# Four graph layers in one kernel: prefix products over two node tiles, a new order of weight tiles at unit boundaries, and copies moved to ScalarE

## The chip, the cores and the metric

The kernel runs on one core of a Trainium2 chip. A core has five engines that work side by side, each on its own queue of instructions: PE (TensorE, matrix products, results in PSUM), DVE (VectorE), ACT (ScalarE, activation functions and copies), POOL (GpSimd) and SP (SyncE). In this kernel SP and POOL issue most of the DMA transfers. Engines wait for each other through semaphores. The metric is the device time of one execution in microseconds (us). Before the change it is 3477.88 us, the median of 3 runs (3473.75 to 3479.8).

## The reference, cut to what matters

There are N = 3327 nodes with 512 features and an adjacency matrix of 0 and 1. Four layers follow each other; each adds its result to its input and normalises every row.

```python
# layers 0, 2 (8 heads of 64) and 3 (4 heads of 128): graph attention
Wh = x @ W                                     # per head
e = leaky_relu(f1[:, :, None] + f2[:, None, :], 0.2)   # f1, f2: Wh times a1, a2
masked = where(adj > 0, e, -9e15)
h = softmax(masked, axis=-1) @ Wh              # layers 2 and 3: then elu
# layer 1: mean over the first 64 neighbours of each node
keep = Ab & (cumsum(Ab, axis=1) <= 64)
nb_mean = (keep @ X) / max(cnt, 1)
y = leaky_relu(X @ W_line.T + b_line) + where(cnt > 0, leaky_relu(nb_mean @ W_nb.T + b_nb), 0)
# after each layer
x = layernorm(x + layer(x))
```

## The kernel before, in words

Nodes are cut into NT = 26 tiles of P = 128 rows; two halves of HALF = 13 tiles (IW = 1664 nodes) are the output halves of an attention layer. The adjacency matrix is loaded once, transposed, and kept on chip as the tile `mask` (one byte for each entry). It arrives in 104 pieces of 128 x 832 integers, which `mask_steps` loads and `mask_set` (line 518) turns into bytes; the first `EARLY` = 88 pieces are handled while layer 0 projects its input, the other 16 beside the first units of layer 0's attention, three in five on DVE and two in five on ACT.

**Projection.** For each tile, `project1` (line 251) transposes the input and `project2` (line 260) multiplies it with W. The products of W with the attention vectors stand in the last columns, so f1 and f2 come out of the same product; ACT copies them into the tile `fc` (line 269). `prepare` (line 293) makes from them, for half of the nodes at a time, a row vector per head (`rd` in memory, over PE transposes `pr` and copies `rr`) and the columns `qc`, `sc` and `bi`; `cut` (line 317) makes bf16 pieces for the sums of the softmax.

**Attention** is done in units (`unit`, line 355): one output half, and one quarter s of the features. In layers 0 and 2 a quarter holds two heads (HS = 2), in layer 3 one (HS = 1). A layer has 8 units. A unit goes over the 26 source tiles j. For each j and each head, DVE makes one weight tile t (line 402, `max` of the row vector `rb` and a column, times the mask) and ACT makes from it a one-byte tile y with a sigmoid (line 405). PE multiplies t with the values `vj` into four banks `po` (line 411), and three tiles later y with `sden` into two banks `pd`, which give the softmax's sums (line 371). Weight tiles have 3 buffers for each head, y tiles 4 (in layer 0 one fewer). The row vectors `rb` of layers 0 and 2 have three buffers; the two of the next unit are loaded by POOL (line 350) as buffers come free.

At the unit's end the four po banks are copied to `ob`, the first by DVE and the others by ACT (lines 426 to 429); four transposes and copies to memory are handed as jobs to the next unit, which does one job after each j. At the end of a half, pd is copied to `db` by both engines (lines 457 to 459), and one of the jobs, `reciprocals` (line 461), multiplies it on PE (`pe`) and takes reciprocals on DVE (lines 474 to 477). Jobs of the first unit of a layer also hold `prepare` and `cut` of the second half.

**Layer 1** is `sage` (line 578). First the input is multiplied with both matrices; the result for the neighbours is cut into three bf16 parts (`zs`, `zl`). Then, for 13 blocks of two output tiles, every pair of block and source tile needs the mask of the first 64 neighbours. ACT writes the count carried from earlier tiles (`cy`, loaded by POOL for four tiles at a time) into one of two PSUM banks `pk` (line 694). PE adds the prefix count of the tile, a product of a triangle of ones with 256 columns of the mask (line 702), and DVE keeps the entries with a count of at most 64 (line 706, `kt`). The kept tiles of the next block are made between the products of this one, ten of them in its first half. PE sums kt times the three parts into `acc` (line 734).

**What sets the order.** PE's instructions run as they are written. On the other engines a planner orders them by estimated costs and due times; an instruction given to `keep_in_program_order` holds its place. Buffers of a pool come free when their last reader is done.

## Time and profile before

| what | value |
| --- | --- |
| median of 3 runs | 3477.88 us |
| the profiled execution | 3476.22 us, its span 3474.4 us |
| busy in the span: PE, DVE, ACT, POOL | 3320.6, 2699.8, 2387.0, 213.3 us |
| mean granted clock of PE | 0.98 |
| line 402, DVE, weight tiles t | 1040, 1959.5 us |
| line 405, ACT, sigmoids y | 1040, 1771.6 us |
| line 411, PE, products po | 8320 records, 1934.8 us |
| line 734, PE, products acc | 645.8 us in two groups |
| lines 694, 702, 706: ACT, PE, DVE on pk | 338 each, 124.0, 92.3, 140.8 us |

All these are from one execution that the hardware profiler recorded. The span runs from its first to its last instruction. A busy time is the time in which an engine had an instruction in work; instructions of one engine can overlap, since PE is pipelined, and a product of 32-bit numbers leaves two records. Behind a group the profile gives the idle time of its engine just before it, and what ended most of it, with an arrow. In a timeline the same stands in brackets. Projection of layer 0 lasts to about 150 us, its attention to about 985, layer 1 to about 1815, layer 2's attention to about 2620, projection and attention of layer 3 to the end.

### The profile page before, as it was taken

The page shows a single profiled execution, that of the slowest core. Times are in us where ns is not written, and L with a number is a line of the kernel's source. Part 1 is how long each engine was busy: PE and PEld are TensorE (multiplying, and loading weights), DVE is VectorE, ACT ScalarE, POOL GpSimd, SP SyncE. Part 2 cuts the span into 40 slices and gives each one's busy share as a digit, 9 for nine tenths or more (in the row PEclk, how much of TensorE's full clock was granted, in tenths as well). Part 3 has the DMA queues.
Part 4 walks back from the last instruction along what each step waited for, and adds up shares of the span by engine and source line. Part 5 has one row for each costly group of instructions (what it writes and reads, how often), then busy time and mean ns, then how long its engine had stood idle before and what let it go on. Part 6 is the DMA issues. An engine that isn't in the chain of part 4 may idle for free.

```text
span 3474.4 us, 48117 instructions
## 1 busy us (share of the span) xinstructions
PE 3320.6 (96%) x18873; PEld 1700.4 (49%) x18926; DVE 2699.8 (78%) x2771; ACT 2387.0 (69%) x2324; POOL 213.3 (6%) x340
## 2 busy tenths in 40 slices
PE   8799999999989999999989999999998999999997
PEld 6544444444444455545554444444446655555553
DVE  6699999999957544344349999999997766668886
ACT  1388988999953343443328999899997655558885
POOL 3100000000010111111110000000001000000000
PEclk9899999999989999999999999999999999999998
DMA  9722111110133422222220111111106511112211
GB/s 382 284 86 68 50 48 47 47 49 28 37 121 122 136 82 68 75 67 69 73 78 18 48 49 47 51 46 43 39 28 205 176 33 44 40 46 91 83 37 47
DMA packets 205354, 276.67 MB, mean 80 GB/s; under 512 B 19325, under 2 KB 140359, under 8 KB 205128
## 3 DMA queue, kind: packets, MB, share of 16 engines
q1 hardware_dynamic: 173464, 164.97, 14.5%
q0 software_dynamic: 26720, 102.65, 9.3%
q10 hardware_dynamic: 4944, 5.98, 0.5%
q8 instruction: 149, 2.44, 0.3%
q14 instruction: 77, 0.63, 0.1%
HBM read 204.92 MB, written 68.60 MB: 79 GB/s over the span
## 4 chain that ended last, share of the span: by engine, by line
PE 59%; issue 27%; DVE 6%; DMA 5%; ACT 2%; POOL 1%; ACTq 0%; POOLq 0%; SPq 0%; DVEq 0%
PE po L411 33%; PE acc L734 9%; PE pd L371 4%; PE pw L265 4%; DVE t L402 3%; DMA raw<-in_adjT_dram 3%; PE pz L623 3%; PE pi L626 2%; PE pt L435 1%; ACT y L405 1%; DMA cy<-ctd 1%; PE pk L702 1%; DVE kt L706 1%; PE pe L466 1%; PE pt L254 1%
## 5 line engine op out<-in xcount | busy, mean ns | idle before, releaser
L402 DVE SCALAR_TENSOR_TENSOR t<-rb,qc,mask 128x1664 f32<-128x1664 f32 x1040 | 1959.5, 1944 | 191.7 <-PE po L411 154.4
L405 ACT ACTIVATE y<-t,bi,sc 128x1664 fp8e4<-128x1664 f32 x1040 | 1771.6, 1766 | 339.1 <-PE pd L371 324.5
L411 PE MATMUL po<-t,vj 128*64 128x448 f32 (+3 forms) x8320 | 1934.8, 521 | 23.8 <-DVE t L402 23.5
L411 PEld LDWEIGHTS po<-t,vj 128*64 128x64 f32 (+1 forms) x8320 | 856.4, 148 | 972.8 <-issue 676.3
L734 PE MATMUL acc<-zs,kt 128*128 128x512 bf16 x1314 | 394.7, 380 | 1.5
L265 PE MATMUL pw<-wsb,xT 128*128 128x264 f32 (+1 forms) x1248 | 301.8, 397 | 18.6 <-DVE vt L271 15.6
L734 PEld LDWEIGHTS <-kt 128*128 128x128 fp8e4 x2028 | 198.2, 98 | 226.4 <-issue 29.8
L694 ACT CAST pk<-cy 128x256 f32<-128x256 bf16 x338 | 124.0, 374 | 268.2 <-DVE kt L706 220.5
L265 PEld LDWEIGHTS pw<-wsb,xT 128*128 128x128 f32 x1248 | 240.7, 197 | 62.9 <-issue 14.1
L371 PE MATMUL pd<-y,sden 128*32 128x448 fp8e4 (+1 forms) x4160 | 259.7, 342 | 10.5 <-ACT y L405 10.5
L706 DVE SCALAR_TENSOR_TENSOR kt<-pk,mask 128x256 fp8e4<-128x256 f32 x338 | 140.8, 420 | 157.2 <-PE pk L702 156.6
L734 PE MATMUL acc<-zl,kt 128*128 128x512 bf16 x661 | 251.1, 380 | 1.4 <-DMA zl<-zd 0.8
L371 PEld LDWEIGHTS <-sden 128*32 128x32 bf16 x4160 | 117.7, 96 | 162.4 <-issue 139.7
L269 ACT COPY fc<-pw 128x8 f32<-128x8 f32 (+1 forms) x156 | 23.6, 162 | 148.2 <-PE pw L265 148.2
L271 DVE TENSOR_TENSOR vt<-pw,dc 128x256 f32<-128x256 f32 x156 | 58.7, 417 | 80.8 <-ACT dc L266 76.6
L350 POOL DMA_DIRECT2D rb<-r x40 | 21.2, 532 | 1617.0 <-DVE t L402 1610.2
L702 PE MATMUL pk<-mask,upto 128*128 128x256 fp8e4 x338 | 92.3, 273 | 19.9 <-ACT pk L694 18.9
L526 DVE TENSOR_SCALAR mask<-raw 128x832 fp8e4<-128x832 int32 (+2 forms) x98 | 58.4, 603 | 51.0 <-DMA raw<-in_adjT_dram 50.7
L623 PE MATMUL pz<-wn,xT 128*128 128x512 f32 x208 | 96.1, 606 | 1.3 <-ACT xT L617 1.3
L626 PE MATMUL pi<-wl,xT 128*128 128x512 f32 x208 | 93.5, 592 | 0.0
L592 POOL DMA_DIRECT2D cy<-ctd x91 | 67.8, 745 | 395.9 <-ACT pk L694 267.8
L714 DVE SCALAR_TENSOR_TENSOR y<-acc,cnt,bnb 128x512 f32<-128x512 f32 x26 | 19.5, 751 | 83.5 <-PE acc L734 83.5
(167 smaller groups left out, 1750.7 us busy)
## 6 DMA issues: line engine op xcount, KB each, us to landing
vj<-v SPq DMA_DIRECT2D x312, 128.0 KB
rb<-r POOLq DMA_DIRECT2D x40, 832.0 KB, 4.7
raw<-in_adjT_dram SPq DMA_DIRECT2D x71, 416.0 KB
cy<-ctd POOLq DMA_DIRECT2D x78, 256.0 KB, 3.9
h<-hd SPq DMA_DIRECT2D x65, 256.0 KB
hd<-hb SPq DMA_DIRECT2D x60, 256.0 KB
v<-vt SPq DMA_DIRECT2D x50, 256.0 KB
xr<-x POOLq DMA_DIRECT2D x45, 256.0 KB, 3.2
```

The lines of the kernel that those rows point to most:

```text
L265: nc.tensor.matmul(pw[e][:, :FW + H], xT[:, c, :], wsb[:, c, e, :], start=c == 0, stop=c == FC - 1)
L371: nc.tensor.matmul(pd[c][32 * kk:32 * kk + 32, :w_], lhsT, rhs, start=(kk, c) not in seen, skip_group_check=final is not None, stop=last a ...
L402: nc.vector.scalar_tensor_tensor(t, rb[k], self.qc[:, j, h:h + 1], mask[:, j, i0:i0 + IW], op0=ALU.max, op1=ALU.mult)
L405: nc.scalar.activation(y, t, AF.Sigmoid, bias=self.bi[:, j, h:h + 1], scale=self.sc[:, j, h:h + 1], saturate=False)
L411: nc.tensor.matmul(po[c][k * D:(k + 1) * D, :z - a_], vj[:, j % 2, k * D:(k + 1) * D], ts[k][:, a_:z], start=j == 0, stop=j == NT - 1)
L592: nc.gpsimd.dma_start(out=cy[:, :n, :], in_=ctd[t:t + n, b * GW:(b + 1) * GW] .rearrange("(o t) i -> o t i", o=1).to_broadcast([P, n, GW]))
L623: nc.tensor.matmul(pz, xT[:, c, :], wn[:, c, :], start=c == 0, stop=c == FC - 1)
L626: nc.tensor.matmul(pi, xT[:, c, :], wl[:, c, :], start=c == 0, stop=c == FC - 1)
L694: nc.scalar.copy(pks[k % 2], carry[b, t // 4 * 4][:, t % 4, :])
L702: nc.tensor.matmul(pk, upto, mask[:, t, i0:i0 + GW], start=False, stop=True, skip_group_check=True)
L706: nc.vector.scalar_tensor_tensor(kt, pk, NEIGHBOURS, mask[:, t, i0:i0 + GW], op0=ALU.is_le, op1=ALU.mult, saturate=False)
L734: nc.tensor.matmul(acc, kts[t][:, s * P:(s + 1) * P], zs(t, c) if c < 2 else zl[:, t, :], start=t == 0 and c == 0, stop=t == NT - 1 and c ...
```

## The change

- **Prefix products for two tiles at once.** In `sage`, a pk bank holds two tiles next to each other; copy, product and selection work on 128 x 512 instead of 128 x 256, and there are 169 of each instead of 338. The pool of kt has half as many buffers of twice the size. Ahead of need, pairs are made after every fourth tile in a block's first half and every second in its second.
- **Order of heads.** In layers 0 and 2, for the first two and the last two source tiles of a unit, both weight tiles of head 0 are made before both of head 1. Between them the order stays.
- **Copies by ScalarE.** In layers 0 and 2, ACT does all four ob copies and all four db copies.
- **Sums and reciprocals.** The products pe are a job of their own, and the reciprocals follow two tiles later, with their first multiplication on DVE held in program order. In the last unit of all, pe is put into a po bank and stands behind the first two groups of transposes.
- **f1 and f2 in place.** The tile fc is gone; the copies go to rc and qc, and prepare works there.
- **Second half's preparation.** In layers 0 and 2, two empty jobs stand ahead of prepare and cut of the second half, and their first DVE instructions are held in program order.
- **The mask's start.** 82 instead of 88 pieces are handled in the projection. The first 8 pieces, not 4, are loaded through ACT's queue, and the four weight tiles of `attend` have four buffers there.
- **The last stores** go from the highest tile of each group to the lowest.

```diff
@@ project2, prepare, cut @@
-                nc.scalar.copy(self.fc[:, t, e * H:(e + 1) * H], pw[e][:, FW:FW + H])
+                nc.scalar.copy((self.rc, self.qc)[e][:, t, :], pw[e][:, FW:FW + H])
...
-            nc.vector.tensor_scalar(rc, f1, RCLAMP, -RCLAMP, op0=ALU.min, op1=ALU.max)
+            ins = nc.vector.tensor_scalar(rc, rc, RCLAMP, -RCLAMP, op0=ALU.min, op1=ALU.max)
+            if pinned:
+                tc.keep_in_program_order(ins)
...
-                nc.vector.tensor_copy(pc[:, :, :, c0], dc)
+                ins = nc.vector.tensor_copy(pc[:, :, :, c0], dc)
+                if pinned:
+                    tc.keep_in_program_order(ins)
@@ unit @@
+            def weights(j, k):
+                h = heads[k]
+                t = tp.tile([P, IW], F32, name="t")
+                nc.vector.scalar_tensor_tensor(t, rb[k], self.qc[:, j, h:h + 1],
+                                               mask[:, j, i0:i0 + IW], op0=ALU.max, op1=ALU.mult)
+                y = yp.tile([P, IW], F8, name="y")
+                nc.scalar.activation(y, t, AF.Sigmoid, bias=self.bi[:, j, h:h + 1],
+                                     scale=self.sc[:, j, h:h + 1], saturate=False)
+                return t, y
...
+                if HS == 1 or j not in (1, NT - 1):
+                    made = {}
+                    for k in range(HS):
+                        for j_ in (j, j + 1) if HS > 1 and j in (0, NT - 2) else (j,):
+                            made[j_, k] = weights(j_, k)
+                ts, ys = zip(*(made[j, k] for k in range(HS)))
...
-                if c:
+                if c or HS == 2:
                     nc.scalar.copy(ob[:, a_:z], po[c][:, :z - a_])
...
-                nc.vector.tensor_copy(db[64:, c * (WB // 2):(c + 1) * (WB // 2)], pd[c][64:, :WB // 2])
+                (nc.scalar.copy if HS == 2 else nc.vector.tensor_copy)(
+                    db[64:, c * (WB // 2):(c + 1) * (WB // 2)], pd[c][64:, :WB // 2])
...
-            return jobs[:2] + [reciprocals] + jobs[2:]
+            if final and s == NS - 1:
+                take = []
+                return [lambda: take.append(transposed(*QUADS[0])), lambda: take.append(transposed(*QUADS[1])),
+                        sums, reciprocals] + [lambda q=q: take[q]() for q in range(2)] + \
+                    [lambda q=q: transposed(*q)() for q in QUADS[2:]]
+            return jobs[:2] + [sums, nothing, reciprocals] + jobs[2:]
@@ sage @@
-                    tc.tile_pool(name="sb_k", bufs=NT + 10, reuse_waits="tile") as kp, \
+                    tc.tile_pool(name="sb_k", bufs=NT // 2 + 5, reuse_waits="tile") as kp, \
...
-                pks = [pkp.tile([P, GW], F32, name=f"pk{i}") for i in range(2)]
+                pks = [pkp.tile([P, 2, GW], F32, name=f"pk{i}") for i in range(2)]
...
-                order = [(b, t) for b in range(len(blocks)) for t in range(NT)]
+                order = [(b, t) for b in range(len(blocks)) for t in range(0, NT, 2)]
...
-                        nc.scalar.copy(pks[k % 2], carry[b, t // 4 * 4][:, t % 4, :])
+                        nc.scalar.copy(pks[k % 2], carry[b, t // 4 * 4][:, t % 4:t % 4 + 2, :])
...
-                    nc.tensor.matmul(pk, upto, mask[:, t, i0:i0 + GW], start=False, stop=True,
+                    nc.tensor.matmul(pk, upto, mask[:, t:t + 2, i0:i0 + GW], start=False, stop=True,
                                      skip_group_check=True)
                     carry_in(k + 1)
-                    kt = kp.tile([P, GW], F8, name="kt")
-                    nc.vector.scalar_tensor_tensor(kt, pk, NEIGHBOURS, mask[:, t, i0:i0 + GW],
+                    kt = kp.tile([P, 2, GW], F8, name="kt")
+                    nc.vector.scalar_tensor_tensor(kt, pk, NEIGHBOURS, mask[:, t:t + 2, i0:i0 + GW],
                                                    op0=ALU.is_le, op1=ALU.mult, saturate=False)
...
-                            if not last and (len(ahead) < 10 and t % 2 == 1 and b > 0 if s == 0 else
-                                             len(ahead) < min(NT, t + 11)):
-                                ahead.append(kept(b + 1, len(ahead)))
+                            if not last and (len(ahead) < 10 and t % 4 == 1 and b > 0 if s == 0 else
+                                             len(ahead) < min(NT, t + 10) and t % 2 == 1):
+                                ahead += kept(b + 1, len(ahead))
@@ the end of layer 3 @@
-                    for q in range(qs.start, qs.stop):
+                    for q in reversed(range(qs.start, qs.stop)):
@@ layer 0 @@
-            EARLY = 3 * NT + 10
-            msteps = mask_steps(rw0, pieces[:EARLY], 5, (), False, 4)
+            EARLY = 3 * NT + 4
+            msteps = mask_steps(rw0, pieces[:EARLY], 5, (), False, 8)
...
-                wt = pool.tile([P, F], F32, name="wt", tag=tag)
+                wt = pool.tile([P, F], F32, name="wt", tag=tag, bufs=FC if tag == "wt" else 1)
...
-                return [lambda: L0.prepare(f0, 1, "xr", 1), lambda: L0.cut(f0, 1, "h", 2)] + count_jobs(pool, 0)
+                return [lambda: None] * 2 + [lambda: L0.prepare(f0, 1, "xr", 1, True), lambda: L0.cut(f0, 1, "h", 2, True)] + \
+                    count_jobs(pool, 0)
```

Layer 2's first jobs change in the same way as layer 0's. In the tail, `final` returns its DVE and ACT part as a function `take` for the last unit, so that it can be called after the reciprocals.

## The prediction

> **What bounds the kernel now.** I read the windows first (busy time of each engine by stage), because the page's PE share of 96% is an average over stages with different limits. Columns: length, then busy us (instructions) of PE, weight loads, DVE, ACT, POOL; granted clock; DMA share; GB/s. The rows are the projection of layer 0, the first unit of its attention, a unit of layer 2, the mean layer (layer 1), a unit of layer 3.
>
> ```profile
> 50.00:150.00 100.00, 86.54 (x411) 71.68 (x409) 64.81 (x149) 21.16 (x88) 24.55 (x40) 0.97 1.01 380
> 150.00:200.00 50.00, 38.46 (x267) 14.87 (x269) 46.46 (x54) 30.14 (x22) 1.07 (x3) 0.83 0.27 78
> 2030.00:2130.00 100.00, 98.17 (x692) 44.63 (x690) 99.35 (x55) 92.02 (x60) 1.06 (x2) 1.00 0.14 44
> 1600.00:1700.00 100.00, 96.58 (x471) 52.58 (x479) 44.00 (x107) 41.49 (x95) 14.08 (x21) 1.00 0.25 74
> 3020.00:3105.00 85.00, 85.00 (x334) 42.73 (x333) 56.20 (x34) 48.38 (x32) 0.53 (x1) 1.00 0.14 42
> ```
>
> So the projection is held by DMA (share 1.01), the mean layer and layer 3 by PE. In layers 0 and 2 both PE and DVE read full, and DVE's order in time decides which it is. It shows a unit boundary as copy, wait, then 52 weight tiles without a hole:
>
> ```profile
> 2020.74 0.61 DVE L429 COPY ob<-po 128x448 f32<-128x448 f32 x1
> 2022.00 96.94 DVE L402 SCALAR_TENSOR_TENSOR t<-rb,qc,mask 128x1664 f32<-128x1664 f32 x52 [0.66 <-DMA rb<-r]
> 2118.86 0.61 DVE L429 COPY ob<-po 128x448 f32<-128x448 f32 x1
> 2120.13 96.94 DVE L402 SCALAR_TENSOR_TENSOR t<-rb,qc,mask 128x1664 f32<-128x1664 f32 x52 [0.65 <-DMA rb<-r]
> ...
> 2235.11 0.21 DVE L474 TENSOR_TENSOR rec<-pe,rc 128x52 f32<-128x52 f32 x1 [2.38 <-PE pe L466]
> ```
>
> A weight tile takes 96.94/52 = 1.865 us of DVE, two tiles of nodes 7.46. PE needs 5.9 for their products and 0.9 for their sums, 6.8, and follows. ACT's timeline has four sigmoids in 6.77, 88 us a unit, and with the copies 92. So layers 0 and 2 are DVE's: each DVE microsecond taken away there is a microsecond, until PE or ACT is reached some 5 us a unit lower.
>
> In the mean layer PE is full except where the prefix product waits for ScalarE to put the carried counts into its bank:
>
> ```profile
> 1366.03 0.38 PE L734 MATMUL acc<-zl,kt 128*128 128x512 bf16 x1
> 1367.37 0.27 PE L702 MATMUL pk<-mask,upto 128*128 128x256 fp8e4 x1 [0.96 <-ACT pk L694]
> 1367.48 0.59 PE L734 MATMUL acc<-zs,kt 128*128 128x512 bf16 x2
> ```
>
> An acc product starts 0.215 after the one before it. Here 1.34 pass, so 1.13 are lost; with three smaller holes beside it (0.10, 0.17, 0.19) a block of 46.1 us loses 1.59.
>
> **The change, part by part** (minus is a gain).
>
> *Copies leave DVE in layers 0 and 2.* The ob copy keeps DVE 0.54 (2118.86 to the wait; 0.61 with its overlap). 14 units are followed by another of their layer: 14 x 0.54 = 7.6. The two db copies between the halves, 1.06 (1.03 and a gap), twice: 2.1. Together -9.7. At each layer's end nothing overlaps: two db copies join ScalarE's row, about 0.95 (its own pair there takes that), twice: +1.9. A boundary gives ScalarE 0.5 more, 92.5 against some 97: hidden.
>
> *Order of heads.* The second row vector of a unit is loaded into the buffer that head 0 of the unit before leaves. Between its last use and its need lie today two weight tiles, the copy and the wait: 2 x 1.865 + 0.54 + 0.65 = 4.9, which is what the load takes (4.7 to landing). In the new order two tiles of the old unit and two of the new lie between, 7.5, so the waits go: 0.69, 1.65, 0.68, 0.22 in layer 0 and 0.37, 0.66, 0.65, 0.81 in layer 2: -5.7. What is late instead is PE: the last but one tile and the next unit's first get their second head one weight tile (1.865) later. PE's wait is hidden as long as the six weight buffers last; the third rival prices this.
>
> *Sums apart from reciprocals.* DVE stood 2.66 (layer 0) and 2.38 behind the pe products, with all weight tiles queued behind it. The reciprocals come two tiles later and are held in program order, when pe is long done: -5.0. PE's 26 products (3.35) stay and are inside its slack. In layer 3 DVE has slack: nothing.
>
> *Six mask pieces leave the projection.* 6 x 426 kB = 2.56 MB, at the 0.40 MB per us of its saturated rows 6.4 us. Loading the fourth weight tile without a buffer wait lets PE start earlier (today it waits for that load 8.40 at 19.79), but DMA is full anyway. Bounds 0 (then PE, busy 87%, is the pace) and -8 (the first 10 us moved 254 GB/s and fill up too); nearer the row of bytes: -5. The pieces come back in layer 0: three more on DVE at 0.50, +1.5, and three on ScalarE at 0.9, hidden.
>
> *Second half's preparation pinned behind six weight tiles.* Today DVE does some 5 us of it before layer 0's first weight tile and PE stands 9.35; it then stalls 3.47 on PE in layer 0 and 0.60 in layer 2. Afterwards that work lies between weight tiles: the same DVE time, a shorter hole on PE. Against it stand two things. ScalarE now needs Exp between sigmoids: two table switches per layer. The trace's row is
>
> ```profile
> L405 ACT ACT_TABLE_LOAD x35 | 44.9, 1283 | 15.2 <-DVE t L402 8.7 <-PE pd L371 5.9
> ```
>
> that is 2 x 1.28 = 2.6 a layer. [...] The trace has the first sigmoid 0.02 after the load's end (158.02 + 1.28, next at 159.32), so I take the row. And three of the four rr copies now stand nearly in a row, each behind the store of the one before (2.76 in layer 0); no sigmoid between them. ScalarE then lags some 12 us behind DVE; six buffers (11.2) and the 5 us of preparation on DVE just cover that. Its four stores move two slots down SP's queue, behind vj loads that have four buffers; their rows are read three units later. [...] Bounds -4 (both stalls gone) and +8 (ScalarE's lag uncovered); taken -1, as the row of the stall is the nearest.
>
> *Pairs in the mean layer.* A 256-column product starts 0.108 before its successor (1363.72 to 1363.83), a 512-column acc 0.215, so 338 x 0.108 = 169 x 0.215: PE gains nothing by itself. The copies and selections halve in number (ACT 0.374 to about 0.56, DVE 0.42 to about 0.7, by the 512-wide rows of this page), off the path. What counts is the loop copy, product, selection on one of two banks. Today it has 1.51 us (two tiles) and needs 0.37 + 0.27 + 0.42 and gaps, 1.2 to 1.3; a table load with the Sqrt (1.58) or an output step breaks it. With pairs it has 3.0 and needs 1.9, so 1.1 of slack for 0.25. Of 1.59 lost per block some 0.6 stay: 11 x 1.0 = 11, and 1 in the first four products. The first block also waits for the carries' DMA (cy, 3.9 to landing, two buffers); that stays. Bounds 0 and -18; taken -12.
>
> *The rest.* f1 and f2 in place: as many copies, same width: 0. Layer 3 has HS = 1, its order and copies stay: 0. The end: transposes ahead of the pe products (fill PE's 1.10 wait, push pe by 0.9), stores reversed so that the two-part last tile isn't the last: -0.5, between -2 and +1.
>
> Sum: -9.7 + 1.9 - 5.7 - 5.0 - 5.0 + 1.5 - 1.0 - 12.0 - 0.5 = **-35.5**. The profiled execution took 3476.2 (span 3474.4 and 1.8 around it), 1.7 under the median of 3477.9; I take the sum off the median: **3442**.
>
> **Rivals.** *Holes stay in the mean layer.* The carry loads or the table loads remain what ends the wait, and pairs only make it coarser. For it: cy waits are 45.4 us of ScalarE's; against it: they lie mostly in the first block. Price +12: 3454.
>
> *ScalarE takes over in layers 0 and 2.* Its sigmoids already wait for PE's release of the y buffers, 324.5 us in all, and every copy moved lands in its row. If it can't catch up after a boundary, the gain of copies, rows and reciprocals (-20.4 + 1.9 = -18.5) is given back: 3461. Against it: 92 busy of 100.
>
> *Slower: PE late at every boundary.* Count from the start of a unit's last four weight tiles. PE starts tile 24 at 5.6, ends tile 25 at 5.6 + 2 x 2.92 = 11.4, the last sums at 13.1 to 13.8, the next unit's tile 0 (complete at 13.1) at 16.0 to 16.7, tile 1 at 18.9 to 19.6. DVE needs the buffer of tile 1's first head for its twelfth weight tile, at 11 x 1.865 = 20.5. So 0.9 to 1.6 are left; what PE is later, DVE loses, 14 times. To turn -35.5 into a loss it takes 35.5/14 = 2.5 us beyond that slack. What could do it: in some units of layer 0 the ob copies stand ahead of the last sigmoid on ScalarE, whose y the last sums need. At 3 us beyond: 3442 + 42 = 3484.
>
> *Nothing to see:* the first two rivals together and the stage's start failing, about 3475.
>
> **How the numbers follow.** As forecast 0.71 (own range 3430 to 3450), mean layer 0.12, ScalarE 0.10, nothing 0.03, PE at boundaries 0.04. Low end: every part at its good bound, -9.7 + 1.9 - 5.7 - 5.0 - 8 - 4 - 18 - 2 = -50.5, the masks' 1.5 hidden in it: 3427. High end 3461, through the first rival to the second. A change under 0.2% (7 us) can't be told from none here. Faster 0.93, same 0.03, slower 0.04.
>
> **What would show it.** DVE's timeline in layers 0 and 2: units of 52 x 1.865 = 97.0 end to end with no ob and no rb wait between (98.1 today), no wait on pe. Projection's last mask near 143 instead of 150. Blocks of 45 instead of 46.1 in the mean layer and no pk wait near 1 us. Layer 3 units at 83 as before. It is wrong if DVE shows waits for PE or ACT after each boundary, if pk still waits, or if layer 0's first unit is longer than its 114 (156 to 270) by more than the 6.5 us of work moved into it.

## The result, and the profile after

The changed kernel takes 3434.9 us (median of four runs, 3434.6 to 3437.3); the kernel before, run beside it, 3478.3 (four runs). The ratio is 0.9879, with an interval from 0.9862 to 0.9896: 43.4 us less. The forecast was 3442, between 3427 and 3461. The profiled executions took 3434.62 (span 3432.9) and 3476.22 (span 3474.4), so the spans differ by 41.5.

The forecast's terms can be sorted by stage and set beside what each stage gave. The stages are cut in the timelines by the first and the last weight tile of a layer (t), and in the mean layer by the first acc product and the first and last output row. The third column is a second profile of the unchanged kernel, described below: it tells how far a stage repeats.

| stage | before, us | before once more | forecast | changed kernel |
|---|---|---|---|---|
| start to layer 0's first t | 156.0 | -2.8 | -10.0 (5 of it only moved) | -11.5 |
| layer 0, first to last t | 813.5 | -2.2 | -5.0 (with 5 moved in) | -8.4 |
| to the mean layer's first acc | 225.4 | -2.5 | +1.0 | -7.1 |
| first acc to first output row | 26.1 | +1.5 | -1.0 | **+7.0** |
| first to last output row | 579.4 | +0.2 | -11.0 | -14.2 |
| to layer 2's first t | 19.2 | -0.7 | 0 | -0.6 |
| layer 2, first to last t | 792.7 | +0.3 | -10.0 | -12.5 |
| to layer 3's first t | 137.7 | +0.3 | +1.0 | **+5.1** |
| layer 3, first to last t | 684.4 | 0.0 | 0 | **+2.6** |
| to the end | 40.1 | -0.3 | -0.5 | -1.9 |
| sum | 3474.4 | -6.2 | -35.5 | -41.5 |

(The forecast for layer 0 is -3.8 for ob copies, -1.0 for db copies, -3.2 for row waits, -2.7 for pe, +1.5 for masks, -0.8 of the one microsecond for the preparation, and +5 for what moves in; for layer 2 it is -3.8, -1.0, -2.5, -2.4 and -0.2.) So the sum was nearly right, but three stages lost 14.7 us where the forecast had zero for the three together, and the others gained 56.2 where it had 35.5.

The windows of the changed kernel (columns as before: length, busy us and instructions of PE, weight loads, DVE, ACT, POOL; granted clock, DMA share, GB/s), for the projection, layer 0's start, a unit of layer 2, the mean layer and a unit of layer 3:

```profile
50.00:140.00 90.00, 78.08 (x370) 63.77 (x369) 58.82 (x134) 19.55 (x79) 24.13 (x38) 0.96 1.03 390
140.00:190.00 50.00, 40.53 (x276) 17.57 (x276) 48.66 (x59) 36.05 (x29) 1.26 (x3) 0.90 0.33 103
1990.00:2090.00 100.00, 99.94 (x706) 47.51 (x704) 100.00 (x55) 93.46 (x63) 1.06 (x2) 1.00 0.14 44
1575.00:1675.00 100.00, 99.22 (x466) 52.24 (x465) 40.36 (x74) 37.92 (x68) 15.36 (x22) 1.00 0.27 77
2968.00:3051.00 83.00, 83.00 (x328) 41.71 (x327) 53.28 (x31) 46.55 (x30) 0.53 (x1) 1.00 0.14 43
```

The bounds are where they were. In layer 2 DVE now reads exactly 100 of 100, and ScalarE 93.5 with the copies (92.0 before). PE in the mean layer is full to 99.2 (96.6 before). DVE's timeline of layer 2 shows the boundaries gone altogether:

```profile
1811.25 383.75 DVE L398 SCALAR_TENSOR_TENSOR t<-rb,qc,mask 128x1664 f32<-128x1664 f32 x206
2194.92 0.20 DVE L493 TENSOR_TENSOR rec<-pe,rc 128x52 f32<-128x52 f32 x1
...
2201.70 363.26 DVE L398 SCALAR_TENSOR_TENSOR t<-rb,qc,mask 128x1664 f32<-128x1664 f32 x195
```

206 weight tiles over four boundaries take 383.75, that is 1.863 each, with no wait in brackets; the reciprocals start without waiting for pe. A unit is 52 x 1.863 = 96.9, as forecast (97.0). Layer 0's first unit, into which 6.5 us of work moved, takes 114.6 (112.5 before), and the projection's last mask step starts at 143.97 (forecast: near 143). And in a block of the mean layer the pk product stands in line with no wait, where 0.96 was lost before:

```profile
1384.87 0.38 PE L759 MATMUL acc<-zl,kt 128*128 128x512 bf16 x1
1385.08 0.38 PE L727 MATMUL pk<-mask,upto 128*128 128x512 fp8e4 x1
1385.30 0.59 PE L759 MATMUL acc<-zs,kt 128*128 128x512 bf16 x2
```

Most blocks take 44.8 to 45.1 (46.1 before; forecast 45). Between the first and the last output row two waits for pk are left, 0.80 and 0.45, where there were twelve of 0.96 or more before. The page's two rows for the pairs (mean ns of one after "busy,") are 0.587 and 0.688, near the 0.56 and 0.7 that were estimated:

```profile
L719 ACT CAST pk<-cy 128x512 f32<-128x512 bf16 x169 | 98.4, 587 | 289.3 <-DVE kt L731 231.5
L731 DVE SCALAR_TENSOR_TENSOR kt<-pk,mask 128x512 fp8e4<-128x512 f32 x169 | 116.1, 688 | 109.2 <-PE pk L727 108.5
```

### The profile page after: what moved, and what is told of

Its sections match the earlier page's. It is cut to its first block, busy times and chain, and to the rows that moved or that the text cites. A ratio compares the mean times of both kernels' runs of the same rounds, so it can differ in the third digit from the quotient of the medians.

```text
span 3432.9 us, 47500 instructions
## 1 busy us (share of the span) xinstructions
PE 3298.5 (96%) x18757; PEld 1660.5 (48%) x18757; DVE 2670.2 (78%) x2575; ACT 2378.1 (69%) x2182; POOL 213.4 (6%) x340
## 4 chain that ended last, share of the span: by engine, by line
PE 71%; issue 13%; DMA 7%; DVE 5%; ACT 3%; POOL 1%; SPq 0%; POOLq 0%; ACTq 0%; DVEq 0%
PE po L421 49%; PE pd L373 7%; PE acc L759 4%; DVE t L398 3%; DMA raw<-in_adjT_dram 3%; PE pz L648 3%; PE pi L651 3%; DMA cy<-ctd 3%; PE pw L264 2%; ACT y L401 1%; PE pt L445 1%; DMA h<-hd 1%; POOL cy L617 1%; PE pa L957 0%; PE pe L480 0%
## 5 line engine op out<-in xcount | busy, mean ns | idle before, releaser
L421 PE MATMUL po<-t,vj 128*64 128x448 f32 (+3 forms) x8320 | 1913.9, 521 | 25.1 <-DVE t L398 24.8
L421 PEld LDWEIGHTS po<-t,vj 128*64 128x64 f32 (+1 forms) x8320 | 835.4, 148 | 975.0 <-issue 713.0
L759 PE MATMUL acc<-zs,kt 128*128 128x512 bf16 x1352 | 405.2, 382 | 0.0
L719 ACT CAST pk<-cy 128x512 f32<-128x512 bf16 x169 | 98.4, 587 | 289.3 <-DVE kt L731 231.5
L264 PEld LDWEIGHTS pw<-wsb,xT 128*128 128x128 f32 x1248 | 240.8, 197 | 56.2 <-issue 5.3
L731 DVE SCALAR_TENSOR_TENSOR kt<-pk,mask 128x512 fp8e4<-128x512 f32 x169 | 116.1, 688 | 109.2 <-PE pk L727 108.5
L268 ACT COPY rc<-pw 128x8 f32<-128x8 f32 (+1 forms) x78 | 12.7, 163 | 142.6 <-PE pw L264 142.6
L651 PE MATMUL pi<-wl,xT 128*128 128x512 f32 x208 | 93.5, 592 | 0.0
L551 DVE TENSOR_SCALAR mask<-raw 128x832 fp8e4<-128x832 int32 (+2 forms) x95 | 55.5, 594 | 44.8 <-DMA raw<-in_adjT_dram 44.5
L256 DVE TENSOR_REDUCE xsum<-xT 128x4 f32<-128x512 f32 x78 | 53.0, 681 | 39.2 <-ACT xT L255 38.8
```

Source lines behind the costliest of these rows:

```text
L264: nc.tensor.matmul(pw[e][:, :FW + H], xT[:, c, :], wsb[:, c, e, :], start=c == 0, stop=c == FC - 1)
L421: nc.tensor.matmul(po[c][k * D:(k + 1) * D, :z - a_], vj[:, j % 2, k * D:(k + 1) * D], ts[k][:, a_:z], start=j == 0, stop=j == NT - 1)
L651: nc.tensor.matmul(pi, xT[:, c, :], wl[:, c, :], start=c == 0, stop=c == FC - 1)
L719: nc.scalar.copy(pks[k % 2], carry[b, t // 4 * 4][:, t % 4:t % 4 + 2, :])
L731: nc.vector.scalar_tensor_tensor(kt, pk, NEIGHBOURS, mask[:, t:t + 2, i0:i0 + GW], op0=ALU.is_le, op1=ALU.mult, saturate=False)
L759: nc.tensor.matmul(acc, kts[t][:, s * P:(s + 1) * P], zs(t, c) if c < 2 else zl[:, t, :], start=t == 0 and c == 0, stop=t == NT - 1 and c ...
```

## The experiments

Questions: does each part give its term, why does the mean layer's start lose 7, and where do layer 3's losses come from? The theory is the forecast's: layers 0 and 2 are DVE's, every DVE microsecond taken away is a microsecond, the mean layer is PE's. The rivals are ScalarE or a late PE at the boundaries.

| run | median, us | kernel before beside it | ratio (interval) |
|---|---|---|---|
| e_pairs | 3465.2 | 3477.2 | 0.9967 (0.9952 to 0.9981) |
| e_heads | 3469.7 | 3477.2 | 0.9975 (0.9968 to 0.9983) |
| e_copies | 3476.9 | 3477.2 | 1.0000 (0.9991 to 1.0008) |
| e_sums | 3474.4 | 3477.2 | 0.9993 (0.9985 to 1.0002) |
| e_headcopy | 3459.2 | 3474.5 | 0.9962 (0.9947 to 0.9977) |
| e_start | 3473.4 | 3474.5 | 0.9996 (0.9987 to 1.0005) |
| e_unpin | 3440.6 | 3474.5 | 0.9908 (0.9892 to 0.9925) |
| e_carry | 3429.7 | 3475.8 | 0.9868 (0.9853 to 0.9882) |
| e_best | 3429.4 | 3475.8 | 0.9865 (0.9850 to 0.9880) |
| e_best_end | 3431.2 | 3475.8 | 0.9872 (0.9856 to 0.9889) |
| e_five | 3458.1 | 3475.8 | 0.9949 (0.9934 to 0.9964) |

Beside the first four, 37 runs of the kernel before spread from 3471.1 to 3487.7. A part worth 3 us is therefore read from the stages of its trace, and the time only has to agree.

### The kernel before, once more

The same program, unedited.

> The kernel before, once more, to see how far its stages repeat. Between the last weight tile of layer 2 and the first of layer 3 its profile had 137.7 us; the changed kernel and the four kernels with one part of the change each had 140.4 to 142.8, though most of them change nothing there. If these stages scatter from one execution to the next, this profile has some other number between 137 and 143; if each program has its own, 137.7 comes back, and so do 202.5 from the mean layer's first product to its first acc product and 684.4 for layer 3's weight tiles.

One run, 3470.0 us. Its stages are the third column of the table above. Those that hang on DMA scatter by 2 to 3 us (the projection, layer 0, the passage to the mean layer); the passage to layer 3 came back as 138.0, layer 3 as 684.4. So the kernel before repeats in these two, and +5.1 and +2.6 are more than its scatter; the changed kernel was profiled once.

### Pairs alone

```diff
-                pks = [pkp.tile([P, GW], F32, name=f"pk{i}") for i in range(2)]
+                pks = [pkp.tile([P, 2, GW], F32, name=f"pk{i}") for i in range(2)]
...
-                order = [(b, t) for b in range(len(blocks)) for t in range(NT)]
+                order = [(b, t) for b in range(len(blocks)) for t in range(0, NT, 2)]
...
-                        nc.scalar.copy(pks[k % 2], carry[b, t // 4 * 4][:, t % 4, :])
+                        nc.scalar.copy(pks[k % 2], carry[b, t // 4 * 4][:, t % 4:t % 4 + 2, :])
```

> Before with the pairs of the mean layer alone. The prediction's term: 12 us faster, all of it between the mean layer's first and last output rows (578.7 us apart before), because a block loses 0.6 instead of 1.6. What the trace of the changed kernel suggests instead: 14 us are gained between these rows (564.5), and some 7 are lost ahead of the first of them, because ScalarE's pairs put the load of the third group of carried counts ahead of layer 2's weights on POOL's queue: then this kernel is about 7 us faster in all, its first output row comes 33 us after its first acc product (26.1 before), and the two loads of wsb are issued after the first pk product, not 18 us ahead of it. If the 7 us come from another part of the change, this kernel is 14 us faster and its first output row comes at 26.

12.0 us faster by the medians (6.6 to 16.7 by the interval). From the first output row to the last 15.3 less, from the first acc product to the first row 6.0 more (26.1 to 32.0). Both halves of the second reading hold; together the two stages give 9.3, and the time alone cannot tell 7 from 12. PE's timeline of this run at the start of the mean layer has two large waits:

```profile
1195.96 0.58 PE L734 MATMUL acc<-zl,kt 128*128 128x512 bf16 x1 [5.20 <-DMA zl<-zd]
1207.37 0.38 PE L702 MATMUL pk<-mask,upto 128*128 128x512 fp8e4 x1 [3.16 <-ACT pk L694]
```

So the pairs themselves bring the loss at the start; which mechanism, e_carry decides.

### Order of heads alone

```diff
-                for k, h in enumerate(heads):
-                    t = tp.tile([P, IW], F32, name="t")
...
+                if HS == 1 or j not in (1, NT - 1):
+                    made = {}
+                    for k in range(HS):
+                        for j_ in (j, j + 1) if HS > 1 and j in (0, NT - 2) else (j,):
+                            made[j_, k] = weights(j_, k)
+                ts, ys = zip(*(made[j, k] for k in range(HS)))
```

> Before with the order of heads at a unit's ends alone. The prediction's term: 5.7 us faster; the waits of DVE for rb (5.7 us in eight boundaries of layers 0 and 2) are gone, all else as before, the ob copy and the pe waits too. Rival (PE late at boundaries): what rb gave comes back as waits of DVE for PE (po) after each boundary, and the time is the same or longer.

7.5 us faster (5.9 to 11.1 by the interval). Layer 0 is 4.0 shorter and layer 2 1.9: 5.9 against 5.7. No wait for rb is left and no wait for PE follows a boundary, so the rival falls. One thing grew: DVE's stall on PE in the first unit is 4.1 in layer 0 and 1.6 in layer 2 (3.5 and 0.6 in the first profile of before, 1.9 and 1.0 in the second), because PE's first pair of weight tiles is complete one tile later.

### Copies alone

```diff
-                if c:
+                if c or HS == 2:
                     nc.scalar.copy(ob[:, a_:z], po[c][:, :z - a_])
...
-                nc.vector.tensor_copy(db[64:, c * (WB // 2):(c + 1) * (WB // 2)], pd[c][64:, :WB // 2])
+                (nc.scalar.copy if HS == 2 else nc.vector.tensor_copy)(
+                    db[64:, c * (WB // 2):(c + 1) * (WB // 2)], pd[c][64:, :WB // 2])
```

> Before with the ob and db copies of layers 0 and 2 on ScalarE alone. The prediction's term: 9.7 less 1.9 = 7.8 us faster. But the row vector's load now has 0.54 us less between its buffer's release and its need, as the copy stood between: if the load is what ends the wait, the eight rb waits grow by 0.54 each and the rest of the boundaries get one, and of 7.6 us at most 3 show; then this kernel is 2 to 4 us faster. If ScalarE takes over, DVE waits for y or for PE after each boundary and nothing shows.

0.3 us faster, between 3.1 faster and 2.8 slower: the term of 7.8 did not come. DVE's timeline of this run at two boundaries of layer 2:

```profile
2009.03 7.53 DVE L402 SCALAR_TENSOR_TENSOR t<-rb,qc,mask 128x1664 f32<-128x1664 f32 x4
2017.46 96.94 DVE L402 SCALAR_TENSOR_TENSOR t<-rb,qc,mask 128x1664 f32<-128x1664 f32 x52 [0.89 <-DMA rb<-r]
2115.55 5.68 DVE L402 SCALAR_TENSOR_TENSOR t<-rb,qc,mask 128x1664 f32<-128x1664 f32 x3 [1.16 <-PE po L411]
```

The first and the last row are cut by the window. The copy is gone and the wait behind it is longer (0.66 before at the first of the two). Over eight boundaries, four in each layer, waits grew from 6.0 to 9.9 us, half of the 7.6 that the ob copies took. The row vector arrives when it arrives, and the copy had been part of the wait for it. (At the second boundary PE's release of a weight buffer came last.) Layers 0 and 2 are 1.2 and 1.9 shorter, so the copies did give 3.1 there; the passage to layer 3 is 3.1 longer, and why is open. Whether ScalarE would allow the full gain is left to the next run.

### Heads and copies together

The two edits above.

> Before with the order of heads and the ob and db copies on ScalarE, both. Alone, the order of heads gave 7.5 us and the copies 0.3. If the copies' gain was held back only by the row vector's load (the new order gives it 7.5 us), DVE now has neither wait nor copy at a boundary of layers 0 and 2: from a layer's first to its last weight tile layer 0 takes 813.5 - 3.2 - 3.7 - 1.0 = 805.5 and layer 2 792.7 - 2.5 - 3.7 - 1.0 = 785.5, and the kernel is 13 to 15 us faster. If ScalarE is what holds the copies back, the two only add: 8 us faster, with waits for y or po at the boundaries.

15.3 us faster by the medians (8.0 to 18.4 by the interval). Layer 0 takes 805.5, as expected; layer 2 783.1, for which 785.5 was expected. Its DVE timeline runs over four boundaries of layer 2 without a wait:

```profile
1826.65 389.36 DVE L396 SCALAR_TENSOR_TENSOR t<-rb,qc,mask 128x1664 f32<-128x1664 f32 x209 [1.53 <-PE po L419]
2217.20 0.21 DVE L483 TENSOR_TENSOR rec<-pe,rc 128x52 f32<-128x52 f32 x1 [1.18 <-PE pe L475]
```

The copies, worth 0.3 alone, are worth 15.3 - 7.5 = 7.8 behind the new order. That this equals the forecast's -9.7 + 1.9 is partly luck: the two intervals are wide, and by the stages layers 0 and 2 are 4.0 and 7.7 shorter than with the order alone. Of these 11.7 us 1.7 are a shorter wait for pe (1.92 and 1.18 where the order alone has 2.38 twice), so some 10 are the copies'. In layer 2 no weight tile waits for ScalarE, and in layer 0 such waits grow by 0.6, so that rival falls.

### Sums apart from reciprocals, alone

```diff
-            def reciprocals():
+            def sums():
...
+            def reciprocals():
+                pe = held[0]
...
+                    tc.keep_in_program_order(
+                        nc.vector.tensor_tensor(r_[:, :, k, ss], pv[:, :, 0, k, ss], rc[:, :, k, ss], op=ALU.mult))
...
-            return jobs[:2] + [reciprocals] + jobs[2:]
+            return jobs[:2] + [sums, nothing, reciprocals] + jobs[2:]
```

> Before with sums and reciprocals as two jobs, two slots apart, and the reciprocals pinned (layers 0, 2 and 3; the end of layer 3 keeps its order). The prediction's term: 5.0 us faster (waits of 2.66 in layer 0 and 2.38 in layer 2 are gone). Rival: the wait is only moved, to the first weight tile behind it, because PE is 3.35 us of sums behind: then the same time, with waits for po in its place.

2.8 us faster (5.2 faster to 0.7 slower). Layer 0 is 2.35 shorter and layer 2 2.51, both waits for pe are gone and no new one stands there: 4.9 of 5.0. But layer 3 is 2.5 longer, where the forecast had zero. Two things make this up. At the boundary behind the second unit of its second half PE waits longer for the last sigmoid. ScalarE's order differs there: between its last two activations of the tile e (line 185) it makes one sigmoid, and before it made two. PE's timeline of the kernel before, and of this run:

```profile
3270.91 0.54 PE L371 MATMUL pd<-y,sden 128*32 128x448 fp8e4 x6 [0.92 <-ACT y L405]
```

```profile
3268.24 0.54 PE L371 MATMUL pd<-y,sden 128*32 128x448 fp8e4 x6 [1.78 <-ACT y L405]
```

That is 0.86. The other 1.7 are a stretch at a lower granted clock just behind the pe products (5 us at 0.66 lose 5 x 0.34): the next eight products po take 4.73 there, and 3.04 in the kernel before, where the clock reads 1.00. The windows of this run, and of e_best where the split is undone in layer 3, at the same place (last three columns: clock, DMA share, GB/s):

```profile
3280.00:3285.00 5.00, 5.00 (x18) 2.27 (x17) 2.61 (x5) 1.32 (x1) 0.20 (x1) 0.66 0.18 52
```

```profile
3240.00:3245.00 5.00, 5.00 (x24) 2.52 (x24) 3.48 (x6) 2.74 (x2) 0.20 (x1) 1.00 0.25 79
```

### Projection's start alone

```diff
-            EARLY = 3 * NT + 10
-            msteps = mask_steps(rw0, pieces[:EARLY], 5, (), False, 4)
+            EARLY = 3 * NT + 4
+            msteps = mask_steps(rw0, pieces[:EARLY], 5, (), False, 8)
...
-                wt = pool.tile([P, F], F32, name="wt", tag=tag)
+                wt = pool.tile([P, F], F32, name="wt", tag=tag, bufs=FC if tag == "wt" else 1)
```

> Before with the projection's start alone: six mask pieces later, eight loads from ScalarE's queue, a buffer for each tile of transposed weights. The prediction's terms: layer 0's first weight tile 5 us sooner (151 in place of 156; between 156 and 148), the layer 1.5 longer by three more mask pieces on DVE: 3.5 us faster. The changed kernel's first weight tile came at 144.5, of which the preparation that it moved behind it explains some 5; so 149.5 would be the rest.

1.1 us faster (4.5 faster to 1.7 slower). The first weight tile comes at 150.4, 5.6 sooner than in the first profile of before and 2.8 sooner than in the second; layer 0 is then 1.0 or 3.2 longer. The sign and the rough size hold; with stages that scatter by 3 us the exact term is not to be had from one trace.

### The preparation where it was

```diff
-                return [lambda: None] * 2 + [lambda: L0.prepare(f0, 1, "xr", 1, True), lambda: L0.cut(f0, 1, "h", 2, True)] + \
-                    count_jobs(pool, 0)
+                return [lambda: L0.prepare(f0, 1, "xr", 1), lambda: L0.cut(f0, 1, "h", 2)] + count_jobs(pool, 0)
...
-                L2.attention(rp, lambda pool, half, s: [lambda: None] * 2 +
-                             [lambda: L2.prepare(mp, 1, "rr", 1, True), lambda: L2.cut(mp, 1, "pc", 1, True)]
+                L2.attention(rp, lambda pool, half, s: [lambda: L2.prepare(mp, 1, "rr", 1), lambda: L2.cut(mp, 1, "pc", 1)]
```

> The changed kernel with the second half's preparation of layers 0 and 2 where it stood before (next to the first weight tiles, not pinned). The prediction's term: 1 us slower, with 4 slower (DVE's stall of 3.5 on PE in layer 0's first unit and of 0.6 in layer 2's is back) and 8 faster (ScalarE's lag behind the pinned preparation) as its bounds. The trace of the changed kernel shows no wait in that place, which speaks for 4 slower.

3440.6 us: 5.7 slower than the changed kernel by the medians, 10 by the ratios, whose intervals leave a wide margin. DVE's timeline of this run at the start of layers 0 and 2:

```profile
149.22 14.98 DVE L398 SCALAR_TENSOR_TENSOR t<-rb,qc,mask 128x1664 f32<-128x1664 f32 x8
168.81 1.95 DVE L398 SCALAR_TENSOR_TENSOR t<-rb,qc,mask 128x1664 f32<-128x1664 f32 x1 [4.60 <-PE po L421]
...
1809.18 3.81 DVE L398 SCALAR_TENSOR_TENSOR t<-rb,qc,mask 128x1664 f32<-128x1664 f32 x2 [1.86 <-PE po L421]
```

The stalls are 4.60 and 1.86, not 3.47 and 0.60. In the changed kernel both are zero: 6.5 us, and the stages from the start to layer 0's end and in layer 2 are 5.0 + 1.9 = 6.9 longer here. ScalarE's timeline of the changed kernel tells what the pinned preparation cost there:

```profile
158.05 1.28 ACT L300 ACT_TABLE_LOAD   x1
159.35 0.29 ACT L300 ACTIVATE rc<-rc 128x104 f32<-128x104 f32 x1
159.66 1.28 ACT L401 ACT_TABLE_LOAD   x1
160.95 1.77 ACT L401 ACTIVATE y<-t,bi,sc 128x1664 fp8e4<-128x1664 f32 x1
```

Two loads of 1.28, and after each the next activation starts within 0.02. DVE does not wait for ScalarE in these first units (in the changed kernel neither from 145 to 250 nor from 1785 to 1880).

### The carried counts' load behind the weights

```diff
-                nc.gpsimd.dma_start(out=cb, in_=ctd[NT:NT + 1, :].rearrange("o (t p) -> p (o t)", p=P))
+                cbl = nc.gpsimd.dma_start(out=cb, in_=ctd[NT:NT + 1, :].rearrange("o (t p) -> p (o t)", p=P))
...
-                            load_carry()
+                            with tc.issue_after(cbl.ins) if k == 2 else nullcontext():
+                                load_carry()
```

> The changed kernel with the load of the third group of carried counts queued on POOL behind the two loads of wsb, bnb and cb, as it stood before. In the changed kernel and in the run of the pairs alone it stands ahead of them and is free only when ScalarE has copied two pairs, so the 1 MB of wsb is issued 1.2 us after the first acc product (23 us ahead of it before) and shares the DMA engines with the first zl tiles: PE waits 4.64 for zl and 4.16 for the carried counts. If that is the cause of the 6 to 7 us between the first acc product and the first output row, these come 26 to 28 apart again and the kernel is 5 to 7 us faster, near 3429. If the pairs themselves are (a pair of counts or of masks later), they stay 33 apart.

3429.7 us, 5.2 less than the changed kernel. POOL's timeline of the kernel before, of the changed kernel, and of this run:

```profile
1171.85 0.80 POOL L143 DMA_DIRECT2D wsb<-in_w_dram  x1 [27.93 <-DVE xi L637]
1174.60 0.77 POOL L143 DMA_DIRECT2D wsb<-in_w_dram  x1 [1.95 <-issue]
...
1194.14 0.76 POOL L592 DMA_DIRECT2D cy<-ctd  x1 [7.89 <-ACT pk L694]
```

```profile
1166.14 0.80 POOL L617 DMA_DIRECT2D cy<-ctd  x1 [48.99 <-ACT pk L719]
1169.07 1.51 POOL L143 DMA_DIRECT2D wsb<-in_w_dram  x2 [2.13 <-DVE kt L731]
1170.57 0.55 POOL L695 DMA_DIRECT2D bnb<-in_bn_dram  x1
```

```profile
1143.94 0.80 POOL L143 DMA_DIRECT2D wsb<-in_w_dram  x1 [27.82 <-DVE xi L662]
1146.69 0.77 POOL L143 DMA_DIRECT2D wsb<-in_w_dram  x1 [1.95 <-issue]
...
1164.66 0.76 POOL L617 DMA_DIRECT2D cy<-ctd  x1 [6.34 <-ACT pk L720]
```

In the changed kernel a load of counts stands first whose buffer ScalarE frees only at 1166; the 1 MB of weights behind it was issued 1.2 us after the first acc product (1167.84) instead of 23 ahead of it. PE's waits at the mean layer's start, in the changed kernel and in this run:

```profile
1173.07 0.58 PE L759 MATMUL acc<-zl,kt 128*128 128x512 bf16 x1 [4.64 <-DMA zl<-zd]
...
1184.64 0.58 PE L727 MATMUL pk<-mask,upto 128*128 128x512 fp8e4 x1 [4.16 <-ACT pk L719]
```

```profile
1171.41 0.59 PE L760 MATMUL acc<-zl,kt 128*128 128x512 bf16 x1 [4.67 <-DMA zl<-zd]
...
1182.45 0.38 PE L728 MATMUL pk<-mask,upto 128*128 128x512 fp8e4 x1 [0.90 <-ACT pk L720]
```

From the first acc product to the first row it is 26.4 again (33.1 in the changed kernel). So it is in the two runs built on this edit (26.4 and 26.6), while the two other variants of the changed kernel, without it, have 32.9 (e_unpin) and 31.4 (e_five). By the time alone 5.2 would not be certain, as the two ratios' intervals overlap. The cause is shown, with one correction to the expectation: the wait for zl stays as in the changed kernel, so the weights did not delay the first zl tile. They delayed the counts behind them: the next load of counts is issued at 1172.59 there and lands 11.2 us later, here at 1166.98 and 7.6. PE's wait for them falls from 4.16 to 0.90. After two waits in a row PE also ran the next 17 us at a granted clock of 0.81 (1184 to 1201), where this run has 1.00 from 1182 on. The 3.3 of the wait and the 3.2 of the clock (17 x 0.19) are the 6.6. Why PE waits 4.7 for zl with the pairs and 0.76 without them stays open.

### Layer 3 as before, and the layers' ends as before

The run before, and:

```diff
+                    if HS == 2:
+                        tc.keep_in_program_order(ins)
...
+            if HS == 1:
+                return jobs[:2] + [lambda: (sums(), reciprocals())] + jobs[2:]
             return jobs[:2] + [sums, nothing, reciprocals] + jobs[2:]
```

> As the run before, and in layer 3 sums and reciprocals are one job again and not pinned (its last unit keeps the changed order). Split and pinned they cost layer 3's weight tiles 2.5 us in the run of the split alone (684.4 to 686.9) and 2.6 in the changed kernel. If that is the split's doing, layer 3's weight tiles are back at 684.4 and this kernel is 2.5 us faster than the run before.

3429.4 us: 0.3 less than e_carry, where 2.5 were expected. Layer 3 is back at 684.4 (and PE's wait of 1.78 at 0.92), but the passage from layer 2 to layer 3 took 144.6 in this program (142.5 in e_carry) and the projection 2.2 more. The edit does what it says; in the time it can't be told from none.

Then the second edit on top, which leaves one ob copy and two db copies of a layer's last unit on DVE:

```diff
-                if c or HS == 2:
+                if c or HS == 2 and not ending:
...
-                (nc.scalar.copy if HS == 2 else nc.vector.tensor_copy)(
+                (nc.scalar.copy if HS == 2 and not ending else nc.vector.tensor_copy)(
```

> As the run before, and at the end of layers 0 and 2, where no weight tiles follow, one ob copy and two db copies go back to DVE. The prediction's term: the copies in a row on ScalarE cost 0.95 at each of the two ends, so 1.9 us faster; if they are what makes the passage from layer 2 to layer 3 take 142.8 instead of 137.7, 5 us faster. If that passage is longer for other reasons (the runs of the pairs and of the sums alone, which change nothing there, had 142.1 and 140.4), 0 to 2 us.

3431.2 us, no gain, and the passage to layer 3 still takes 142.8. So the copies in a row on ScalarE are not what lengthens it, and the term of +1.9 for them isn't visible.

### Five weight buffers

```diff
-            with tc.tile_pool(name="at_t", bufs=3 * self.HS, reuse_waits="tile") as tp, \
+            with tc.tile_pool(name="at_t", bufs=3 * self.HS - (self.HS == 2), reuse_waits="tile") as tp, \
```

> The changed kernel with five weight buffers instead of six in layers 0 and 2, to measure how near the rival of a late PE was. By the prediction's count PE has 0.9 to 1.6 us to spare at each of 14 boundaries; one buffer less takes one weight tile, 1.865, away, so 0.3 to 1.0 are short: 4 to 14 us slower, with waits of DVE for po near the twelfth weight tile after a boundary. If the count was too careful, the time stays. If it was not careful enough within a unit, each pair of node tiles waits and the loss is much larger.

23.2 us slower than the changed kernel: layer 0 9.6, layer 2 5.5, and 6 in the passage to the mean layer, where no weight buffer is used and whose cause is open. 15 in the two layers is just above the expected 14. Two boundaries of layer 0 in DVE's timeline of this run, an ordinary one and the one between the halves:

```profile
479.17 1.95 DVE L398 SCALAR_TENSOR_TENSOR t<-rb,qc,mask 128x1664 f32<-128x1664 f32 x1 [0.55 <-PE po L421]
481.31 95.08 DVE L398 SCALAR_TENSOR_TENSOR t<-rb,qc,mask 128x1664 f32<-128x1664 f32 x51 [0.19 <-ACT y L401]
577.76 1.95 DVE L398 SCALAR_TENSOR_TENSOR t<-rb,qc,mask 128x1664 f32<-128x1664 f32 x1 [1.38 <-ACT db L468]
580.56 7.54 DVE L398 SCALAR_TENSOR_TENSOR t<-rb,qc,mask 128x1664 f32<-128x1664 f32 x4 [0.84 <-PE po L421]
```

An ordinary boundary is short by 0.74 here, so with the sixth buffer (1.865) it has some 1.1 to spare: the forecast counted 0.9 to 1.6. Between the halves 2.2 are short, more than the sixth buffer holds, and there the changed kernel does wait in layer 0, 1.2 us in three pieces (0.44, 0.41, 0.33; the last is for a sigmoid of ScalarE). Not all of it is PE: the profile puts the 1.38 to ScalarE's db copies.

## Why the prediction was right, and where it was not

DVE's waits and copies in layers 0 and 2 and PE's holes in the mean layer went as forecast, and they carry the gain. That the sum came so near is in part luck: 14.7 us of losses that nobody forecast stand against 20.7 of gains beyond the forecast, 8.1 of them in the passage to the mean layer.

**Row waits, copies, reciprocals** (-5.7, -9.7 and -5.0): right in mechanism and size, measured as 5.9, some 10 and 4.9 in layers 0 and 2. What the forecast did not say is that the first two hang together. It listed the copy and the wait as two terms, and in the order in which they were taken, heads first, they add. Taken alone, the copies lose half of their gain to the row's load, which fills the gap; that the whole kernel gains nothing then is also due to the passage to layer 3, which is 3.1 longer.

**The pinned preparation** (-1, between -4 and +8): wrong, it gives 6.5 by the waits and 5.7 to 10 by the times, outside the bound of 4 on the good side. The step that failed is "the row of the stall is the nearest": 3.47 and 0.60 were read from the kernel before, but the other edits change that stall (the new order lets PE begin one weight tile later; alone it has 4.09 in layer 0, with the copies 4.88), and without the pinning it is 4.60 and 1.86. The costs weighed against the gain (tables, ScalarE's lag) stayed hidden. No run shows a term of -1, nor any part of the +8; what the traces show in their place is both stalls gone, 6.5 us.

**Pairs** (-12): right in sum for the part alone (12.0 by the medians), by two errors that cancel, which is luck. In the blocks the gain is 14 to 15, some 1.2 for each of twelve block lengths where the forecast had 1.0 for each of eleven; so 0.3 to 0.6 of the 1.59 stayed ("some 0.6 of 1.59" was a little too careful). In the first block, where the forecast said one microsecond would be won, 6 to 7 are lost. The forecast had looked at the counts' DMA ("that stays") and not at POOL's queue: a copy of two tiles frees the counts' buffer at another moment, the planner puts the load that waits for it ahead of the weights, and everything behind it stands. POOL's order is the planner's and is fixed when the kernel is built, so it can be read before a run.

**Layer 3** (zero): 2.6 lost. "In layer 3 DVE has slack: nothing" failed. PE sets the pace there, as the forecast says itself, and it did not ask what else the split would move. In layer 3's second half, first to last weight tile, all fourteen traces take one of four lengths. The nine without the split have 344.2 (seven) or 345.8 to 345.9 (two), the five with it 346.7 (three) or 348.4 (two). PE's wait for the last sigmoid at the boundary behind this half's second unit is 0.91 to 0.92 in all nine and 1.78 in all five: the split's own part is 0.86. What is left of the differences is 1.6 to 1.7 or twice that, and in the changed kernel it is PE's granted clock: from 3240 to 3248 it reads 0.79, which loses 8 x 0.21 = 1.7, and 1.00 over the 192 us before and the 147 after. The kernel before (344.2) reads 1.00 over the whole half. But the lower clock does not go with the split alone. In the 4 us behind the pe products at this boundary it reads 0.57 in the changed kernel, e_sums and e_five, 0.63 in e_unpin and 0.62 in e_heads, which has no split, and 1.00 in the nine others, of which e_carry has it. That the split brings it on is not shown.

**Layers' ends** (+1.9): not seen. The passage from layer 2 to layer 3 is 5.1 longer, yet e_pairs (142.1) and e_sums (140.4) are longer too although each engine's instructions there stand as in the kernel before, e_start (137.7) is not, and undoing the copies doesn't help. The clock may be part of it: over the whole passage its mean is 0.93 before, 0.90 in e_pairs and e_sums and 0.89 in the changed kernel, and 0.04 of 140 us is 5.6. But e_best_end has 0.92 and is as long, and e_start 0.91 and is not. In the changed kernel PE has a granted clock of 0.57 from 10 to 30 us behind the last weight tile, 0.66 before. What sets it stays open, as does the cause of the 7.1 gained in the passage to the mean layer, which no part was meant to give.

**Projection and end** (-3.5 with the masks, -0.5): 1.1 alone within 4.5 faster and 1.7 slower; the end gave 1.9 and was not tried alone.

**Rivals.** Neither ScalarE nor PE took over: ScalarE by e_headcopy, PE by e_five, which shows that it was near; one buffer less costs 15 us in the two layers. The holes did not stay in the mean layer.

The best kernels here are e_carry and e_best, at 3429.7 and 3429.4, which the runs do not tell apart.

## What to carry to other kernels

A copy ahead of a wait may be part of the wait: before counting both as gains, ask when the awaited transfer was issued and whether the copy's time was already given to it. A stall read from the kernel before is the right price only if no other edit moves its two ends. And when an edit changes when a buffer comes free, read every queue that holds a load into that buffer, because what stands behind that load there, though unrelated, moves with it.

## What the runs showed of the hardware

PE's granted clock fell for a few microseconds in the middle of a unit in which PE had work all the time. In the changed kernel's layer 3 the window from 3242.20 to 3245.20 reads 0.50, those from 3238 to 3241 and from 3246 to 3249 read 1.00, and PE is busy in all of each. The same eight products po that take 3.04 in the kernel before take 4.74 here: 1.7 us, as much as the 0.79 of the window from 3240 to 3248 loses.

This was not expected in a full unit. From 3226 to 3246 PE's only wait is one of 1.8. Just ahead of the slower products stand the 26 pe products of 8 columns, 2.96 us; in the kernel before they take 2.96 too, and the 4 us behind them read 1.00. So these products alone do not decide it, and what does is not shown. A difference of 1.7 us between two single traces can be one such stretch, present in one and not in the other.
